# A cap of two on the indirect DMAs under way, and sums in PSUM and sweeps on ScalarE in the last layers of a macaron MoE kernel

## The chip, the cores and the metric

The kernel runs on one core of a Trainium2 chip. The metric is the device time of one execution in microseconds. Twelve runs of the kernel before have a median of 1014.88 us (1011.14 to 1021.59). One further execution was profiled; its lines are what is read below.

The engines are named as the profile names them: PE is TensorE (matmul), PEld its weight load, DVE is VectorE, ACT is ScalarE, POOL is GpSimd, SP is SyncE, which here only issues transfers. An indirect DMA is a transfer whose row numbers are read from a tile; POOL issues it and moves on, and the DMA engines carry it out.

## The reference

The input is 8 batches of 512 tokens with 128 features, all float32. Each token row goes through six residual layers:

```python
x = x + 0.5 * moe(layernorm(x))      # 8 experts, top 2, d_ff 512, relu
x = x + attention(layernorm(x))      # 16 heads of 8, rope, causal, 512 tokens
x = x + 0.5 * moe(layernorm(x))
x = x + 0.5 * fp6_linear(layernorm(x))          # the first fp6 layer
x = x + gated_scan_and_silu_ffn(layernorm(x))   # "mix" below
x = x + 0.5 * fp6_linear(layernorm(x))          # the second fp6 layer
```

`fp6_linear` rounds each block of 32 features to an FP6 grid with one scale per block, multiplies by a quantized 128x128 weight and adds a bias `bq`. `gated_scan_and_silu_ffn` takes u = layernorm(x), normalises it by its root mean square, forms three gates, runs the scan h = a*h + s along the tokens, sets u = u + h, normalises again, and adds a SiLU feed-forward of width 384; the layer's output u + ffn(u) is added to x.

## The kernel before

**Tiles.** A batch is one tile of 128 partitions x 512: four blocks t of 128 tokens, tokens on the partitions and the 128 features along the row. `X[b]` holds the residual of batch b in SBUF from start to end. Eight PSUM banks of 128x512 are shared by everything.

**Mixture of experts.** Stage 0 (before the attention) runs in the groups [0,1], [2,3,4], [5,6,7] of batches, stage 2 (after it) in [0,1], [2,3], [4,5], [6,7]. A group is normalised and routed; POOL then scatters its rows to DRAM, sorted by expert, one indirect DMA per 128 rows and choice (L790, 64 KB each). Expert tiles of 128 rows come back (`xs`), are transposed on PE (L842, `xp`), multiplied by W1 (L853, `hp`), passed through relu (L865, `hs`) and multiplied by W2 (L874, `yp`); DVE adds the bias (L883, `yo`) and SP stores the tile. Each of the 177 tiles loads its expert's weights, 578 KB (L821, `wx`). POOL gathers the results with one indirect DMA per 128 rows and choice (L905, `y`), and DVE adds them to `X[b]` with the gate as weight (L918). There are 128 scatters and 128 gathers.

**Attention.** Scores are formed twice on PE (L1025: `sa` for a maximum that DVE takes at L1077, `sb` for the exponential on ACT at L1088). POOL clears the masked corner (affine select, L1096, `pm`), and PE multiplies by the values (L1132, `av`).

**The tail of a batch** is first fp6 layer, mix, second fp6 layer, and the store of `X[b]` (L1363).

- `normed` (four statistics per tile on DVE at L570, four aggregations at L576, eps added at L577) is followed by a power of -1/2 on POOL (`power`, L588). `scaled_rows` applies it, either on ACT (one DVE product of mean and factor at L599, then four ACT passes of 128x128 at L605) or on DVE (four passes at L609, L611 for the form without a mean).
- `fp6` adds half the bias to `X[b]` (L1267, POOL or DVE), quantizes (`quantized`, L1209 to L1243: twelve DVE or POOL steps, of which L1217, L1233 and L1239 may run on POOL), transposes on PE (L544, `tpq`), copies to SBUF (L531 on ACT, L535 on DVE), multiplies by the weight (L1277, four products into `ypq`) and adds half the product to `X[b]` (L1280, DVE).
- `mix` forms the gates (L1310 on PE, L1312 on ACT), prepares and runs the scan on DVE (L1318, L1320, L1322), transposes h back (four PE transposes at L544 into the bank `ht`), sets u = u + 0.5 h (L1326, DVE), adds u to `X[b]` (L1328, POOL or DVE), normalises u (`root_mean`: four squares on ACT at L556, one DVE step at L559, a power on POOL), and runs the feed-forward (L1337 and L1341 on PE, L1339 on ACT, L1343 on DVE, L1350 on PE into `yom`), whose result DVE adds to `X[b]` (L1356).

**Who sets the order.** Every step is an `Op` with one or more engines that may run it, its estimated costs, the buffers it takes and the steps it needs. `Graph.search` runs a list scheduler 12 times with changing priorities and keeps the best plan; the instructions are then emitted in that order, engine by engine, and each engine's queue runs in the order written. Engines are chosen in the plan, so that a step that may run on POOL or DVE can change sides when anything in the plan changes. `Graph.run` lets at most 8 bulk transfers of a queue be under way; the program itself makes an indirect DMA wait for the one eight before it.

Of the kernel before, what the change touches and what calls it, by code (L numbers as in the profile page):

```python
# [15 lines left out]
P = 128  # L16
# [40 lines left out]
STEP = 4.0  # L57
TURNED = (0,)


# [42 lines left out]
class Op:  # L103

    __slots__ = "alts fn acq bufs deps succ left prio start end eng ready bulk order skew idx pace occ".split()

# [25 lines left out]
class Graph:  # L132
# [4 lines left out]
    def add(self, alts, fn, r=(), w=(), acq=(), deps=(), order=(), bulk=0, skew=0.0, pace=0.0):  # L137
        o = Op()
        o.alts = alts if isinstance(alts, list) else [alts]
        o.fn, o.acq, o.bulk, o.skew, o.pace = fn, list(acq), bulk, skew, pace  # L140
        o.succ, o.start, o.end, o.eng, o.idx = [], None, None, None, len(self.ops)
        needs = {id(d): d for d in deps}
        bufs = {id(b): b for b in acq}
# [25 lines left out]
    def levels(self):  # L169
        for o in reversed(self.ops):  # L170
            e, t, lat, _ = o.alts[0]
            if e == "PE":
                lat = t + 0.3
            if o.bulk:
                lat = 2.2 + o.bulk / 330e3
            o.prio = max(
                [s.prio + (lat if o in s.deps else 0.0) for s in o.succ], default=lat
            ) + o.skew

    def search(self, attending, slots):  # L180
# [18 lines left out]
    def refine(self, order, span, first):  # L199
# [13 lines left out]
        for o, f in zip(self.ops, first):  # L213
            o.prio = MIX * (span - late[id(o)]) + (1 - MIX) * o.prio

    def run(self, attending, slots):
# [46 lines left out]
        while ready:  # L263
            best = []
            low = 1e18
            for o in ready:
# [4 lines left out]
                for alt in o.alts:  # L271
                    e, occ, lat, m = alt
                    st = max(free[e], o.ready, slot_t)
                    if o.bulk and e == "POOL":
                        st = max(st, free[e] + (0.28 if scattering else 0.0))
                    if o.bulk and len(flight[e]) >= 8:
                        st = max(st, flight[e][-8])
                    raw = st
# [68 lines left out]
def kernel(  # L347
# [9 lines left out]
    vecs: bass.AP,  # L357
    bq: bass.AP,
    wq8: bass.AP,
    consts: bass.AP,  # L360
# [125 lines left out]
    half_bq = fixed("half_bq", [P, P])  # L486
    load_late(half_bq, bq.partition_broadcast(P), P * P * 4)
    half_vec = fixed("half_vec", [P, 2])
    wd_t = fixed("wd_t", [P, P])

# [3 lines left out]
    def clear_for_attention(after):  # L494
# [16 lines left out]
        def halves(e):  # L511
            nc.gpsimd.tensor_scalar_mul(half_bq.t, half_bq.t, 0.5)
            nc.gpsimd.tensor_scalar_mul(half_vec.t[:, 0:1], vec_s.t[:, V_BG : V_BG + 1], 0.5)
            nc.gpsimd.tensor_scalar_mul(half_vec.t[:, 1:2], vec_s.t[:, V_BD : V_BD + 1], 0.5)

        add(pool(P, k=2, each=1.3e-3), halves, r=[vec_s], w=[half_bq, half_vec], order=[after])

# [45 lines left out]

    def normed(src, view, name, eps, skew=0.0):

        sm = small(f"sm_{name}")

        def stat(t):
            st = sm.t[:, 0:24].rearrange("p (t k) -> p t k", t=NT)
            nc.vector.bn_stats(out=st[:, t, :], in_=view()[:, t, :])  # L570

        def go(e):
            st = sm.t[:, 0:24].rearrange("p (t k) -> p t k", t=NT)
            mv = sm.t[:, 24:32].rearrange("p (t k) -> p t k", t=NT)
            for t in range(NT):
                nc.vector.bn_aggr(out=mv[:, t, :], in_=st[:, t, :])  # L576
            nc.vector.tensor_scalar_add(sm.t[:, 32:36], mv[:, :, 1], eps)  # L577

        for t in range(NT):
            add(("DVE", 0.2, 0.28, None), lambda e, t=t: stat(t), r=[(src, t)], w=[(sm, t)],  # L580
                acq=[sm] if t == 0 else [], skew=skew)
        add(("DVE", 0.4, 0.5, None), go, w=[sm], skew=skew)
        power(sm, 32, 36, skew)
        return sm
# [51 lines left out]
    def moe_front(s, g):  # L636
# [147 lines left out]
        for n in range(n_b):  # L784
            for k in range(2):
                for t in range(NT):
                    i = n * NT + t

                    def scatter(e, n=n, k=k, t=t, i=i):
# [5 lines left out]
                        )  # L795
                        state["scattered"].append(unordered(ins, f"out{name}"))

                    state["sent"].append(add(
                        ("POOL", 1.02, 2.2, None), scatter, r=[us[n], (keep, f"at{k}"), (rows_in[g], ("s", name, i, k))],
                        bulk=P * P * 4,  # L800
                    ))

    def moe_tiles(s, g):
# [90 lines left out]
    def moe_combine(s, g):  # L894
# [3 lines left out]
        for n, b in enumerate(GROUPS[s][g]):  # L898
            for k in range(2):
                y = buf("g", "y", f"y{k}_{s}_{b}")  # L900
                for t in range(NT):
                    i = n * NT + t

                    def gather(e, y=y, k=k, t=t, i=i):
# [5 lines left out]
                        )  # L910
                        data_from(ins, state["stored"])

                    add(("POOL", 1.02, 2.2, None), gather, r=[(state["keep"], f"at{k}")], w=[(y, t)],
                        acq=[y] if t == 0 else [], deps=state["done"], bulk=P * P * 4)

                def weighed(e, y=y, k=k, n=n, b=b, t=0):
# [343 lines left out]
    def fp6(b, s, sk):  # L1260

        name = f"{s}_{b}"
        y, iz, iv, r = (buf("g", "tail", f"q{k}_{name}") for k in range(4))
        m = normed(X[b], lambda: X[b].t, f"t{name}", 1e-5, skew=sk)
        scaled_rows(y, X[b], lambda: X[b].t, m, acq=[y, iz, iv, r], skew=sk)
        add([pool(S, each=1.7e-3), dve(S, own=True)],
            lambda e: engines[e].tensor_tensor(  # L1267
                X[b].t, X[b].t, half_bq.t.unsqueeze(1).to_broadcast([P, NT, P]), ALU.add),
            r=[half_bq], w=[X[b]], skew=sk)
        quantized(y, iz, iv, r, S // FB, name, small(f"qs_{name}"), skew=sk)  # L1270
# [3 lines left out]

        def go(e):
            for t in range(NT):
                nc.tensor.matmul(yp.t[:, ts(t, P)], iz.t[:, ts(t, P)], wd_t.t, start=True, stop=True)  # L1277

        add(pe(P, NT), go, r=[iz, wd_t], w=[yp], acq=[yp], skew=sk)
        add(dve(S), lambda e: nc.vector.scalar_tensor_tensor(flat(X[b]), yp.t, 0.5, flat(X[b]), ALU.mult, ALU.add),  # L1280
# [5 lines left out]
    def mix(b, sk):  # L1286
        nm = f"{b}"
        u, xn, xnt, s0, s1, s2, h = (buf("g", "tail", f"mix{k}_{nm}") for k in range(7))
        sgs = [s0, s1, s2]
        m = normed(X[b], lambda: X[b].t, f"m{nm}", 1e-5, skew=sk)  # L1290
        scaled_rows(u, X[b], lambda: X[b].t, m, acq=[u, xn, xnt, s0, s1, s2, h], skew=sk)
# [16 lines left out]
        def gate(i, bias, half, n, dst):  # L1308
# [13 lines left out]
        add(dve(2 * S), lambda e: nc.vector.tensor_tensor_scan(h.t, s0.t, s1.t, 0.0, ALU.mult, ALU.add),  # L1322
            r=[s0, s1], w=[h], skew=sk)
        ht = bank(f"ht_{nm}")
        turned(h, lambda: tokens(h), ht, skew=sk)
        add(dve(S), lambda e: nc.vector.scalar_tensor_tensor(u.t, ht.t, 0.5, u.t, ALU.mult, ALU.add),  # L1326
            r=[ht], w=[u], skew=sk)
        add([pool(S), dve(S, own=True)], lambda e: engines[e].tensor_tensor(flat(X[b]), flat(X[b]), u.t, ALU.add),  # L1328
            r=[u], w=[X[b]], skew=sk)
        m2 = root_mean(u, xn, f"n{nm}", 1e-6, skew=sk)  # L1330
# [4 lines left out]
        for f in range(NGF):  # L1335
# [8 lines left out]
                r=[pu], w=[sgs[f]], skew=sk)  # L1344
        yo = bank(f"yom_{nm}")

        def go(e):
            for t in range(NT):
                for f in range(NGF):
                    nc.tensor.matmul(  # L1350
                        yo.t[:, ts(t, P)], sgs[f].t[:, ts(t, P)], wout_s.t[:, f, :],
                        start=(f == 0), stop=(f == NGF - 1),
                    )

        add(pe(P, NT * NGF), go, r=[*sgs, wout_s], w=[yo], acq=[yo], skew=sk)
        add(dve(S), lambda e: nc.vector.tensor_tensor(flat(X[b]), flat(X[b]), yo.t, ALU.add),  # L1356
# [26 lines left out]
    for g in GROUPS[2]:  # L1383
        for b in g:
            tail(b, -STEP * k)
            k += 1

    order = G.search(bursts, SLOTS)
    for o in order:
        for b in o.acq:  # L1390
            where = p_ps if b.kind == "ps" else wk
            b.t = where.tile([P, WIDTH[b.kind]], F32, tag=f"{b.kind}{b.slot}", name=b.name)
        o.fn(o.eng)

# [75 lines left out]
```

## Time and profile before

| | |
|---|---|
| median of 12 runs | 1014.88 us (1011.14 to 1021.59) |
| the profiled execution | 1014.2 us, with a span of 1012.5 us in the trace |
| mean granted clock of TensorE | 0.964 of full speed |
| moved by DMA | 163.61 MB, 162 GB/s mean |
| L905, gathers: one DMA_INDIRECT on POOL | 128 of them, 137.9 us busy |
| L790, scatters: one DMA_INDIRECT on POOL | 128 of them, 131.4 us busy |

The profile's page has the busy time of each engine, the span in 40 slices of 25.3 us with the busy share in tenths, and the chain of work that ended last. Besides the page, four views of the trace are used: the busy time of each engine in chosen stretches of the span; the groups of instructions by line within one stretch; the timeline, instruction by instruction; and the chain in order of time. A group's line gives its count, its busy time in us and the mean ns of one, then the idle time of its engine ahead of it and what ended that.

### The profile page before, as it was taken

How to read it: one execution, taken by the hardware profiler on the slowest of the kernel's cores; microseconds unless marked ns; L12 is line 12 of the kernel's file. 1: busy time of each engine (PE TensorE's matmuls, PEld its weight loads, DVE VectorE, ACT ScalarE, POOL GpSimd, SP SyncE). 2: the span in 40 equal slices, each digit the busy share in tenths (PEclk: the TensorE clock that was granted, in tenths of full speed). 3: DMA queues.
4: the chain of work that ended last, by engine and by line, in shares of the span. 5: the costliest groups of instructions: out<-in, count | busy, mean ns of one | idle time of the engine just before them, and what ended most of it. 6: DMA issues, size and time to landing. Idle time of an engine off the chain costs nothing.

```text
span 1012.5 us, 22544 instructions
## 1 busy us (share of the span) xinstructions
PE 904.5 (89%) x7282; PEld 673.6 (67%) x7282; DVE 739.0 (73%) x2706; ACT 524.6 (52%) x1396; POOL 543.1 (54%) x679
## 2 busy tenths in 40 slices
PE   5488979999999899999999999999998898957973
PEld 5378968776777654656667775665997787534552
DVE  7612364888665699987878668990458869899997
ACT  2144534365666545456656555556555664544641
POOL 3783347267221585475264227783078475775562
PEclk9999998999999979989999999999999999987995
DMA  5779997875554210042343561450899894100001
GB/s 159 263 231 388 361 363 266 285 219 162 181 159 150 70 54 14 22 169 77 117 138 118 151 187 50 147 150 10 278 363 290 266 331 138 34 16 1 22 21 43
DMA packets 102071, 163.61 MB, mean 162 GB/s; under 512 B 11200, under 2 KB 70720, under 8 KB 101952
## 3 DMA queue, kind: packets, MB, share of 16 engines
q1 hardware_dynamic: 93760, 145.37, 43.9%
q0 software_dynamic: 8192, 16.79, 5.0%
q8 instruction: 58, 0.95, 0.4%
q14 instruction: 61, 0.50, 0.1%
HBM read 129.28 MB, written 29.16 MB: 156 GB/s over the span
## 4 chain that ended last, share of the span: by engine, by line
PE 49%; DVE 26%; DMA 8%; POOL 7%; issue 7%; ACT 3%; SPq 1%; POOLq 0%; ACTq 0%; DVEq 0%
PE hp L853 11%; PE yp L874 10%; PE sb L1025 8%; PE sa L1025 7%; PE av L1132 5%; DVE sa L1077 4%; DMA wx<-in_wexp 4%; POOL y L905 3%; DMA y<-rows_out,keep 2%; DVE x L918 2%; POOL rows_in L790 2%; PE lp L670 1%; PE xp L842 1%; DVE q L1241 1%; DVE q L1243 1%
## 5 line engine op out<-in xcount | busy, mean ns | idle before, releaser
L1077 DVE CUSTOM_DVE_ANT_0 sa<-sa,future_s 128x384 f32<-128x384 f32 (+3 forms) x512 | 240.6, 513 | 75.6 <-PE sa L1025 43.8
L865 ACT ACTIVATE hs<-hp,wx 128x128 f32<-128x128 f32 x692 | 196.1, 372 | 141.8 <-PE hp L853 116.2
L1088 ACT ACTIVATE pm<-sb 128x512 f32<-128x512 f32 x320 | 173.2, 598 | 155.5 <-PE sb L1025 79.9
L1096 POOL TENSOR_SCALAR_AFFINE_SELECT pm<-pm 128x256 f32<-128x256 f32 x256 | 107.6, 438 | 190.7 <-ACT pm L1088 189.9
L1025 PE MATMUL sb<-qa,ka 32*128 32x128 f32 (+3 forms) x1024 | 198.8, 467 | 9.0 <-DVE nstat L1077 6.0
L853 PE MATMUL hp<-xt,wx 128*128 128x128 f32 x1416 | 193.7, 283 | 6.4 <-DMA wx<-in_wexp 6.3
L874 PE MATMUL yp<-wx,hs 128*128 128x128 f32 x1416 | 188.2, 278 | 10.4 <-DVE yo L883 8.1
L853 PEld LDWEIGHTS hp<-xt,wx 128*128 128x128 f32 x1416 | 176.4, 196 | 27.5 <-issue 14.5
L1025 PE MATMUL sa<-ka,qm 32*128 32x384 f32 (+3 forms) x1024 | 189.3, 471 | 3.5 <-DVE qm L537 2.3
L874 PEld LDWEIGHTS yp<-wx,hs 128*128 128x128 f32 x1416 | 171.2, 192 | 22.1 <-ACT hs L865 12.3
L905 POOL DMA_INDIRECT y<-rows_out,keep x128 | 137.9, 1078 | 72.3 <-issue 28.8
L790 POOL DMA_INDIRECT rows_in<-um,keep x128 | 131.4, 1027 | 60.3 <-issue 30.6
L1025 PEld LDWEIGHTS sb<-qa,ka 32*128 32x128 f32 x1024 | 100.1, 186 | 46.7 <-DVE nstat L1077 19.0
L1025 PEld LDWEIGHTS sa<-ka,qm 32*128 32x128 f32 x1024 | 87.2, 186 | 28.9 <-issue 3.3
L883 DVE TENSOR_TENSOR yo<-yp,wx 128x128 f32<-128x128 f32 x177 | 49.4, 285 | 65.9 <-PE yp L874 63.7
L1132 PE MATMUL av<-pm,vpad 128*32 128x256 f32 (+3 forms) x1024 | 83.0, 455 | 1.2 <-POOL pm L1096 1.2
L1077 DVE DVE_READ_ACCUMULATOR2_ANT nstat<- 128x1 f32 x512 | 71.5, 140 | 0.0
L1132 PEld LDWEIGHTS av<-pm,vpad 128*32 128x32 f32 x1024 | 29.0, 112 | 60.6 <-issue 38.4
L535 DVE COPY xt<-xp 128x256 f32<-128x256 f32 (+1 forms) x82 | 33.1, 407 | 43.1 <-PE xp L842 43.0
L918 DVE SCALAR_TENSOR_TENSOR x<-y,keep,x 128x128 f32<-128x128 f32 x128 | 49.7, 403 | 14.0 <-DMA y<-rows_out,keep 13.3
L842 PE MATMUL xp<-cst,xs 128*128 128x128 f32 x177 | 35.5, 282 | 13.5 <-DMA xs<-rows_in 12.3
L842 PEld LDWEIGHTS xp<-cst,xs 128*128 128x128 f32 x177 | 22.0, 144 | 18.6 <-issue 14.6
(214 smaller groups left out, 1219.7 us busy)
## 6 DMA issues: line engine op xcount, KB each, us to landing
wx<-in_wexp SPq DMA_DIRECT2D x177, 578.0 KB
xs<-rows_in SPq DMA_DIRECT2D x85, 128.0 KB
rows_out<-yo SPq DMA_DIRECT2D x85, 128.0 KB
rows_in<-zero SPq DMA_DIRECT2D x2, 1984.0 KB
rows_in<-zero SPq DMA_DIRECT2D x2, 1472.0 KB
x<-in_x SPq DMA_DIRECT2D x8, 256.0 KB
rows_in<-um,keep POOLq DMA_INDIRECT x128
y<-rows_out,keep POOLq DMA_INDIRECT x128
```

The costliest lines, as they stand in the source:

```text
L790: ins = nc.gpsimd.indirect_dma_start(out=rows_in[g].t[0 : NTL * TW, :], out_offset=bass.IndirectOffsetOnAxis(ap=at(k)[:, i : i + 1], axis= ...
L842: nc.tensor.transpose(xp.t[:, ts(h, P)], halves(xs.t)[:, h, :], ident)
L853: nc.tensor.matmul(hp.t[:, ts(fc, P)], wx[i].t[:, E_W1 + fc * P : E_W1 + (fc + 1) * P], xt.t[:, ts(h, P)], start=True, stop=True,)
L865: nc.scalar.activation(o, a, AF.Relu, bias=bias)
L874: nc.tensor.matmul(yp.t[:, ts(h, P)], hs[i].t[:, ts(fc, P)], wx[i].t[:, E_W2 + fc * P : E_W2 + (fc + 1) * P], start=(fc == 0), stop=(fc == ...
L905: ins = nc.gpsimd.indirect_dma_start(out=tokens(y)[:, t, :], out_offset=None, in_=rows_out[g].t[0 : NTL * TW, :], in_offset=bass.IndirectO ...
L918: nc.vector.scalar_tensor_tensor(X[b].t[:, t, :], tokens(y)[:, t, :], state["gates"](k)[:, i : i + 1], X[b].t[:, t, :], ALU.mult, ALU.add,)
L1025: nc.tensor.matmul(sc.t[:, at : at + hi - lo], stat.t[rows, ts(m, P)], mov.t[rows, lo:hi], start=True, stop=True,)
L1077: nc.vector.tensor_tensor_reduce(out=sc.t[:, at : at + wd], in0=sc.t[:, at : at + wd], in1=future_s.t[:, S - wd : S], scale=-1.0, scalar=3 ...
L1088: nc.scalar.activation(pm.t[:, (h % 2) * S : (h % 2 + 1) * S], sc.t, AF.Exp, scale=scale)
L1096: nc.gpsimd.affine_select(out=diag, in_=diag, pattern=[[0, 2], [1, P]], compare_op=ALU.is_ge, fill=0.0, base=0, channel_multiplier=-1,)
L1132: nc.tensor.matmul(av.t[32 * j : 32 * j + 32, m * P :], v.t[:, row, :], pm.t[:, at : at + S - m * P], start=first, stop=last,)
```

## The change

**Indirect DMAs.** Every gather, and every scatter but those of the first group of stage 0, is planned with at most two under way (`FLIGHT = 2`), and really waits in POOL's queue for the indirect DMA two before it to have landed.

**Late tails** (batches 4 to 7). In both fp6 layers the bias no longer goes onto `X[b]`: a product of a row of ones with `bq4` (the bias four times, 1x512) opens the bank `ypq`, and the four products accumulate onto it. In the mix, u is put into the bank `ht` by a product of the identity with u (128x512), and four products of h with half the identity accumulate 0.5 h onto it in place of the four transposes; L1326 and L1328 are gone, the second normalisation reads `ht`, the output products (L1350) accumulate onto the same bank, and `X[b]` takes the sum once (L1356). In the first fp6 layer and the mix of these batches ACT, not DVE, adds eps.

**Second fp6 layer** (all eight batches). Mean and variance come from four Copy and four Square passes of ACT with accumulators (`normed_on_act`), one small DVE step before the power and one after it, and four ACT passes apply them (`rows_on_act`). L570, L576, L577 and L599 are gone there.

**The plan** is searched again. `G_BOOST` and `BOOST` hold only zeros. By instructions, from before to after: PE 3940 to 3952, DVE 2708 to 2639, ACT 1366 to 1440, POOL 684 to 668.

```diff
+FLIGHT = 2
+ON_ACT = (5,)
+LATE = (4, 5, 6, 7)
+EPS_ACT = LATE
...
-                    if o.bulk and len(flight[e]) >= 8:
-                        st = max(st, flight[e][-8])
+                    if o.bulk and len(flight[e]) >= o.limit:
+                        st = max(st, flight[e][-o.limit])
...
+bq4 = fixed("bq4", [1, S])
+load_late(bq4, bq4_in, S * 4)
+half_ident = fixed("half_ident", [P, P])
...
+def normed_on_act(src, view, spare, name, eps, acq=(), skew=0.0):
+    sm = small(f"sm_{name}")
+    mean = lambda: mv_of(sm)[:, :, 0]
+    for t in range(NT):
+        add(("ACT", 0.42, 0.55, None), lambda e, t=t: nc.scalar.activation(
+            tokens(spare)[:, t, :], view()[:, t, :], AF.Copy, scale=-1.0 / P, accum_out=sm.t[:, 24 + 2 * t : 25 + 2 * t]),
+            r=[(src, t)], w=[(sm, t), (spare, t)], acq=[sm, *acq] if t == 0 else [], skew=skew)
+    for t in range(NT):
+        add(("ACT", 0.42, 0.55, None), lambda e, t=t: nc.scalar.activation(
+            tokens(spare)[:, t, :], view()[:, t, :], AF.Square, bias=sm.t[:, 24 + 2 * t : 25 + 2 * t],
+            accum_out=sm.t[:, 32 + t : 33 + t]),
+            r=[(src, t)], w=[(sm, t), (spare, t)], skew=skew)
+    add(dve(NT), lambda e: nc.vector.tensor_scalar(
+        sm.t[:, 32:36], sm.t[:, 32:36], 1.0 / P, eps, ALU.mult, ALU.add), w=[sm], skew=skew)
+    power(sm, 32, 36, skew)
+    add(dve(NT), lambda e: nc.vector.tensor_tensor(
+        sm.t[:, 60:64], mean(), sm.t[:, 32:36], ALU.mult), w=[sm], skew=skew)
+    return sm
+
+def rows_on_act(dst, view, sm, skew=0.0, src=None):
+    for t in range(NT):
+        add([("ACT", 0.43, 0.55, None)], lambda e, t=t: nc.scalar.activation(
+            tokens(dst)[:, t, :], view()[:, t, :], AF.Identity, scale=sm.t[:, 32 + t : 33 + t], bias=sm.t[:, 60 + t : 61 + t]),
+            r=[(src, t), sm], w=[(dst, t)], skew=skew)
...
# normed
-            nc.vector.tensor_scalar_add(sm.t[:, 32:36], mv[:, :, 1], eps)
+            if not eps_act:
+                nc.vector.tensor_scalar_add(sm.t[:, 32:36], mv[:, :, 1], eps)
...
+            add(act(NT), lambda e: nc.scalar.activation(sm.t[:, 32:36], mv_of(sm)[:, :, 1], AF.Copy, bias=eps),
+                w=[sm], skew=skew)
...
# scatters, and the same without the condition for gathers
+                    if (s, g) != (0, 0):
+                        state["sent"][-1].limit = FLIGHT
...
# fp6
+            if late:
+                nc.tensor.matmul(yp.t, ones.t[0:1, :], bq4.t, start=True, stop=False, skip_group_check=True)
             for t in range(NT):
-                nc.tensor.matmul(yp.t[:, ts(t, P)], iz.t[:, ts(t, P)], wd_t.t, start=True, stop=True)
+                nc.tensor.matmul(
+                    yp.t[:, ts(t, P)], iz.t[:, ts(t, P)], wd_t.t, start=not late, stop=True, skip_group_check=late)
...
# mix
+            def mixed(e, u=u):
+                nc.tensor.matmul(ht.t, ident, u.t, start=True, stop=False, skip_group_check=True)
+                for t in range(NT):
+                    nc.tensor.matmul(ht.t[:, ts(t, P)], h.t[:, ts(t, P)], half_ident.t,
+                                     start=False, stop=True, skip_group_check=True)
+            u = ht
...
-        yo = bank(f"yom_{nm}")
+        yo = u if late else bank(f"yom_{nm}")
...
# emission
-        o.fn(o.eng)
+        ins = o.fn(o.eng)
+        if o.bulk and o.eng == "POOL":
+            if o.limit < 8:
+                data_from(ins, indirect[-o.limit :][:1])
+            indirect.append(ins)
```

## The prediction

> **What bounds the kernel now.** I read the page's slices first, then the busy times by stretch, then the groups and the timeline of the last stretch.
>
> ```profile
> PE 904.5 (89%) x7282; PEld 673.6 (67%) x7282; DVE 739.0 (73%) x2706; ACT 524.6 (52%) x1396; POOL 543.1 (54%) x679
> ...
> PE   5488979999999899999999999999998898957973
> ...
> DVE  7612364888665699987878668990458869899997
> ```
>
> The mean says PE. The slices say two stages: PE has 9 in nearly all slices from the seventh to the thirtieth, DVE in the last five or six. The table by stretch puts numbers on it (columns: length, then busy PE, PEld, DVE, ACT, POOL; clock, DMA share, GB/s):
>
> ```profile
> 54.00:150.00 96.00, 85.63 (x689) 80.11 (x689) 33.22 (x104) 46.88 (x162) 46.20 (x50) 1.00 0.96 342
> 150.00:420.00 270.00, 261.75 (x2247) 183.78 (x2247) 203.62 (x790) 143.72 (x360) 138.65 (x196) 0.96 0.47 151
> 720.00:860.00 140.00, 129.22 (x1029) 117.73 (x1028) 102.40 (x351) 81.68 (x267) 84.98 (x76) 1.00 0.86 282
> 860.00:1012.50 152.50, 109.48 (x495) 70.68 (x493) 139.54 (x365) 65.99 (x167) 90.84 (x77) 0.86 0.07 23
> ```
>
> Until 860 PE is at 89 to 97% from 54 us on; its idle time there is some 58 us in all, 27 of it in the first 54 us. From 860, when the last expert tile is through, DVE holds the end: 139.5 of 152.5 us. So an edit pays after 860 if it takes DVE time, and costs before 860 if it adds PE time or makes PE wait.
>
> Part of DVE's end stage is not work but stalls beside POOL:
>
> ```profile
> 963.26 1.71 POOL L1328 TENSOR_TENSOR x<-x,mix 128x512 f32<-128x512 f32 x1
> ...
> 963.98 1.28 DVE L1236 TENSOR_SCALAR q<-q 128x512 f32<-128x512 f32 x1
> ...
> 968.21 1.05 POOL L1217 TENSOR_TENSOR q<-q,qs 128x512 f32<-128x512 f32 x1 [0.53 <-DVE qs L1210]
> 968.34 0.95 DVE L577 TENSOR_SCALAR sm_t<-sm_t 128x4 f32<-128x4 f32 x1
> ```
>
> L1236 takes 0.35 us when POOL is quiet and 1.28 beside POOL's addition; the eps step, 0.08 to 0.11 alone, takes 0.95. At each shape's unloaded duration DVE's instructions after the last expert sum come to 115.4 us, against 139.5 busy: 24 us are stalls, over about 35 two-input POOL operations, 0.69 us each. The groups of that stretch show where they land:
>
> ```profile
> L1241 DVE SCALAR_TENSOR_TENSOR q<-q,q 128x512 f32<-128x512 f32 x11 | 9.7, 881 | 1.2 <-POOL q L1239 1.2
> L570 DVE BATCH_NORM_STATS2 sm_t<-x 128x6 f32<-128x128 f32 x36 | 8.9, 276 | 0.0
> L577 DVE TENSOR_SCALAR sm_t<-sm_t 128x4 f32<-128x4 f32 x9 | 6.1, 681 | 0.3
> L1239 DVE TENSOR_TENSOR q<-q,q 128x512 f32<-128x512 f32 x3 | 3.7, 1222 | 0.1
> L1326 DVE SCALAR_TENSOR_TENSOR mix<-ht,mix 128x512 f32<-128x512 f32 x5 | 3.4, 679 | 0.0
> ...
> L1267 POOL TENSOR_TENSOR x<-x,half_bq 128x512 f32<-128x512 f32 x10 | 12.9, 1290 | 10.4 <-ACT q L605 9.4 <-DVE sm_n L559 0.9
> L1239 POOL TENSOR_TENSOR q<-q,q 128x512 f32<-128x512 f32 x8 | 10.5, 1320 | 2.9 <-DVE q L1236 2.8
> ```
>
> **The change part by part.**
>
> *DVE after the last expert sum.* I count instructions in DVE's order behind the last `yo`, before and after the change, at the durations of these groups. Statistics 36 to 11 at 0.25 us (8.9/36): -6.2. Aggregations 36 to 12 at 0.08: -2.0. Eps 13 to 0: -6.8 (6.1 for the fp6 layers, 0.7 for the mix). L599 8 to 2 at 0.245 for the fp6 layers, 5 to 6 for the mix: -1.4. L1326 5 to 0: -3.4. L1328 2 to 0: -1.4. One quantization less behind that point (10 to 9): -5.3. Three L1343, one L1356, one L1280 less: -3.3. Against it: L1239 goes from POOL to DVE, 3 to 9 there, 0.68 us unloaded and 1.22 loaded, +4.1 to +7.3, taken as 5.7; copies L535 0 to 3, +1.8; twelve small steps of the new norm at 0.15, +1.8; L609, L611, L918, L1217, L1233 and L1320 together +1.6. The sum is -18.9. The other way: by unloaded durations the list is 103.5 us instead of 115.4, -11.9, and POOL's two-input operations behind the first gather of that group fall from 36 to 19 (L1267 9 to 2, L1239 7 to 0, L1328 3 to 1, L1233 10 to 8, L1217 7 to 8), 17 x 0.69 = -11.7, together -23.6. If all stalls merely moved to other instructions, only -11.9 would stay. I take -18, with -12 to -24 for the range: when DVE gets thinner its idle time, 9 us of the 149 to its last instruction, grows.
>
> The Trainium skill, "SBUF — State Buffer", section "Who interferes with whom", says that a DVE instruction with two SBUF inputs, or in a two-port mode, contends for a pair of ports with GpSimd, each blocking the other for a whole instruction, and that one with a single SBUF input outside those modes does not. By that rule alone the eps steps, with one SBUF input, would not be held, and taking 13 of them away would be worth 13 x 0.09 = 1.2 us and not 6.8; the row with 681 ns speaks against that, unless such a step runs in one of the two-port modes, which the section does allow it.
>
> *ACT.* For each second fp6 norm ACT gets eight sweeps; L556's, alike, follow each other by 0.29 us: 8 x 0.29 = 2.3 us, where DVE had 4 x 0.20 + 4 x 0.07. In the last stretch six such norms add 14 us and eps some 2 to the 66 of 152: ACT stays at 60%. It lies beside another batch's DVE work, except in the very last tail, where it is in the chain: +1 us (0, or +4 if another tail's eight sweeps and four L605 passes, 2.3 + 1.5, stand ahead of it).
>
> The Trainium skill, "ScalarE: Activation LUTs", gives an ACTIVATE 0.093 us more for each pointer operand. This speaks against the Square and the Identity sweeps; eight such operands more per norm would make 0.7 us more latency each, 0.7 us on the end by its figure.
>
> *PE.* Eight bias products and four identity products of 128x512, 0.95 to 1.02 us each (L1337: 42 records, two a product, in 21.4 us), and sixteen products for sixteen transposes, 0.375 against 0.175 us: +15 us in all. After 860 PE has 43 us idle and this hides there. What counts is the order: at the groups' prices 801.5 us of PE work stood ahead of the last expert product and now 812.1 do, since one batch's feed-forward and products are put ahead. PE's idle time ahead of it can take some; I take +6 (0 to +10.6). DVE work ahead of it is the same, 776.6 and 779.3 us.
>
> *Two indirect DMAs under way.* POOL issues one per 1.30 us and the trace shows how long each flies:
>
> ```profile
> 119.43 1.00 POOL L905 DMA_INDIRECT y<-rows_out,keep  x1 [0.30 <-ACT hs L865]
> ```
> ```profile
> 119.43 6.35 DMA y<-rows_out,keep
> ```
>
> From issue to last packet it is 4.5 to 5.9 us while weights stream (DMA share 0.86 to 1.04) and 1.9 to 2.3 us where DMA is light. With two under way the period is half of that: 2.3 to 3 us loaded instead of 1.3, and still 1.3 when light. Before, four or five flew at once. Queued behind a waiting POOL instruction are the affine selects (L1096, which `av` on PE waits for), powers (L588) and products of the tails. Loaded places: the 16 gathers of stage 0's first group, 114 to 135, which become about 16 x 2.4 = 38 us, so +17 at their end; the 24 scatters at 149 to 184; the scatters and gathers at 736 to 788 and 810 to 834. The last 16 gathers, 866 to 897, run at DMA share 0.07 and are not delayed. PE hides most of it: its order now starts the attention at 127 instead of 107 us of PE work, so the first gathers have 20 us more expert work to hide behind, and the scatters of group 2 are read at 173 instead of 151. The selects have no such cover; I give them 3 us of PE time. Both ends: -2 (the streams of weights get a little more of the wire, 5% of 16 engines' span being indirect) to +16 (nothing hidden at one of the places). I choose near the low end since each place is followed by expert or attention work that PE may take in the written order.
>
> The Trainium skill, "DMA: Bandwidth & Descriptors", section "Anatomy of one DMA", gives 2.0 us plus bytes/436e3 for such a DMA: 2.15 us for 64 KB, so two under way would cost nothing, and this term would be 0. The light rows agree with it; the loaded ones, 6.35 in the chain, do not.
>
> *Fixed costs:* one load of 2 KB and one POOL step more early on, beside streams of 578 KB loads: nothing.
>
> **Sum:** against the profiled execution, 1014.2 - 18 + 1 + 6 + 3 = 1006.2. The median lies 0.7 above that execution; I forecast 1006, with 1000 to 1011 as this case's own range.
>
> **Rivals.**
>
> *The cap starves PE.* At 114 to 150 PE already idles 16% and the whole gain rests on POOL running ahead. If the first gathers' +17 us or the selects behind waiting scatters reach PE, the price is 16 in place of 3 or more, and the end is at 1019; with ACT or the last scatters too, 1023. It decides from the point where POOL's lag passes about 10 us. For it: POOL's waits are real and the planned cost of an indirect DMA is 2.2 us, not 5; PE's order is fixed. Against: the order holds more work ahead of each reader.
>
> *PE becomes the bound and the tail keeps its stalls.* PE gives +10.6, the tail only -12: 1014.2 - 12 + 10.6 + 1 = 1013.8, no difference. For it: L1239 on DVE has two SBUF inputs and meets POOL's L1233.
>
> *The whole tail gain comes, the work ahead is absorbed:* 1014.2 - 24 + 1 + 1 = 992. For it: 17 POOL operations less; PE's 58 us idle.
>
> **How the numbers follow.** My case 0.47; the whole gain 0.15; no difference 0.13; the starved PE 0.25. A measurement tells 0.3% (3 us) from no change. Faster 0.63, same 0.12, slower 0.25. The range leaves out the far parts of both outer cases: 991 to 1021.
>
> **What would show it.** Busy DVE after the last expert sum near 117 to 121 us; L577 gone from the late groups and L1236, L1241 nearer 0.4 and 0.65 us; the last `yp` near 865 (868 or more if the cap costs, 859 if all is absorbed). If indirect DMAs wait long, POOL rows of L790 and L905 show idle time ended by DMA, and PE idle time before `av` ended by POOL's `pm`. I am wrong if PE's idle time ahead of 860 grows by more than 10 us, or if DVE is idle for more than 20 us after it.

## The result

The changed kernel takes 1047.83 us (median of 11 runs, 1040.42 to 1050.43) against 1014.89 us (46 runs): 1.0312 times the time before, 95% interval 1.0293 to 1.0331. I had forecast 1006 us, with a range up to 1021. The profiled execution has a span of 1041.5 us, at a mean granted clock of 0.945 instead of 0.964.

### The profile page after: what moved, and what is told of

The parts are those of the page before. It is cut to its first block, busy times and chain, and to the rows that moved or that the text cites. A ratio compares the mean times of both kernels' runs of the same rounds, so it can differ in the third digit from the quotient of the medians.

```text
span 1041.5 us, 22686 instructions
## 1 busy us (share of the span) xinstructions
PE 920.4 (88%) x7322; PEld 684.2 (66%) x7322; DVE 721.1 (69%) x2637; ACT 548.6 (53%) x1534; POOL 518.9 (50%) x663
## 4 chain that ended last, share of the span: by engine, by line
PE 47%; DVE 17%; DMA 8%; issue 7%; POOL 6%; ACT 3%; SPq 0%; POOLq 0%; DVEq 0%; ACTq 0%
PE yp L925 9%; PE hp L904 9%; PE sb L1078 7%; PE sa L1078 6%; PE av L1185 5%; DVE sa L1130 4%; DMA y<-rows_out,keep 4%; DMA wx<-in_wexp 3%; POOL y L956 3%; ACT pm L1141 1%; DVE x L971 1%; PE xp L893 1%; DVE nstat L1130 1%; DVE q L1287 1%; POOL pm L1149 1%
## 5 line engine op out<-in xcount | busy, mean ns | idle before, releaser
L1078 PE MATMUL sb<-qa,ka 32*128 32x256 f32 (+3 forms) x1024 | 203.1, 479 | 8.5 <-DVE nstat L1130 5.1
L1149 POOL TENSOR_SCALAR_AFFINE_SELECT pm<-pm 128x256 f32<-128x256 f32 x256 | 105.1, 429 | 203.6 <-ACT pm L1141 202.5
L1078 PE MATMUL sa<-ka,qm 32*128 32x384 f32 (+3 forms) x1024 | 192.8, 488 | 2.8 <-DVE nstat L1130 2.5
L925 PE MATMUL yp<-wx,hs 128*128 128x128 f32 x1416 | 186.5, 277 | 5.1 <-DVE yo L934 4.9
L956 POOL DMA_INDIRECT y<-rows_out,keep x128 | 137.0, 1070 | 99.7 <-DMA wx<-in_wexp 34.2
L1078 PEld LDWEIGHTS sb<-qa,ka 32*128 32x128 f32 x1024 | 102.5, 191 | 47.4 <-DVE nstat L1130 15.6
L1078 PEld LDWEIGHTS sa<-ka,qm 32*128 32x128 f32 x1024 | 90.5, 195 | 29.0 <-DVE nstat L1130 6.6
L971 DVE SCALAR_TENSOR_TENSOR x<-y,keep,x 128x128 f32<-128x128 f32 x128 | 49.3, 389 | 63.3 <-DMA y<-rows_out,keep 63.1
L1185 PE MATMUL av<-pm,vpad 128*32 128x256 f32 (+3 forms) x1024 | 85.5, 465 | 4.3 <-DVE nstat L1130 2.6
L550 DVE COPY xt<-xp 128x256 f32<-128x256 f32 (+1 forms) x87 | 35.5, 408 | 37.7 <-PE xp L893 37.0
```

Of the source, the lines that this page charges most:

```text
L925: nc.tensor.matmul(yp.t[:, ts(h, P)], hs[i].t[:, ts(fc, P)], wx[i].t[:, E_W2 + fc * P : E_W2 + (fc + 1) * P], start=(fc == 0), stop=(fc == ...
L956: ins = nc.gpsimd.indirect_dma_start(out=tokens(y)[:, t, :], out_offset=None, in_=rows_out[g].t[0 : NTL * TW, :], in_offset=bass.IndirectO ...
L971: nc.vector.scalar_tensor_tensor(X[b].t[:, t, :], tokens(y)[:, t, :], state["gates"](k)[:, i : i + 1], X[b].t[:, t, :], ALU.mult, ALU.add,)
L1078: nc.tensor.matmul(sc.t[:, at : at + hi - lo], stat.t[rows, ts(m, P)], mov.t[rows, lo:hi], start=True, stop=True,)
L1149: nc.gpsimd.affine_select(out=diag, in_=diag, pattern=[[0, 2], [1, P]], compare_op=ALU.is_ge, fill=0.0, base=0, channel_multiplier=-1,)
L1185: nc.tensor.matmul(av.t[32 * j : 32 * j + 32, m * P :], v.t[:, row, :], pm.t[:, at : at + S - m * P], start=first, stop=last,)
```

## The profile after

The page's engine line and two rows of its 40 slices:

```profile
PE 920.4 (88%) x7322; PEld 684.2 (66%) x7322; DVE 721.1 (69%) x2637; ACT 548.6 (53%) x1534; POOL 518.9 (50%) x663
...
PE   6389289987999989999999999999999888958995
...
PEclk9999699968999999889999999999999999979995
```

PE's fifth slice, 104 to 130 us, stands at 2; the fifth slice of before had 9, and the granted clock drops in the same slice and again in the ninth. The table by stretch (columns as before; the last row begins where the last expert product ends), and the row of the kernel before from its last expert product on:

```profile
54.00:150.00 96.00, 69.92 (x554) 65.61 (x553) 24.34 (x81) 38.89 (x135) 43.93 (x50) 0.89 0.85 285
...
902.00:1041.50 139.50, 108.41 (x469) 68.41 (x467) 113.03 (x296) 74.47 (x253) 67.89 (x59) 0.86 0.07 24
```
```profile
862.60:1012.50 149.90, 106.88 (x477) 68.70 (x476) 137.09 (x358) 64.14 (x163) 90.02 (x76) 0.86 0.07 23
```

The last expert product ends at 902.0 us, before at 862.6: 39.4 us later. From there to the end it takes 139.5 us, before 149.9: 10.4 us less. So the tail is faster, and all of the loss and more lies ahead of it. In the 39 us PE idles 25 us more (90.0 against 65.0 us up to that product) and is busy 14 us longer (812.0 against 797.6). Of the idle time 16 us come before the attention's first score, which starts at 185.4 instead of 149.9 us; the rest of that delay is the 20 us of expert work that the new order puts ahead of the attention.

The 16 us come with one gap of 20.65 us; before, no gap of PE between 104 and 150 us is longer than 2.3 us. PE's timeline, then SP's in the changed kernel, SP's first load of the same rows in the kernel before, and POOL's in the changed kernel:

```profile
101.42 1.95 PE L925 MATMUL yp<-wx,hs 128*128 128x128 f32 x16
124.02 1.11 PE L893 MATMUL xp<-cst,xs 128*128 128x128 f32 x4 [20.65 <-DMA xs<-rows_in]
```
```profile
106.07 0.43 SPq L427 DMA_DIRECT2D wattn_s<-in_wattn  x1
...
107.69 0.55 SPq L478 DMA_DIRECT2D rows_in<-zero  x1
108.28 9.57 SPq L427 DMA_DIRECT2D half_bq<-in_bq  x1
...
119.50 1.93 SPq L882 DMA_DIRECT2D xs<-rows_in  x4
...
134.93 2.23 SPq L872 DMA_DIRECT2D wx<-in_wexp  x2
```
```profile
94.14 0.38 SPq L831 DMA_DIRECT2D xs<-rows_in  x1
```
```profile
82.10 0.98 POOL L838 DMA_INDIRECT rows_in<-um,keep  x1 [0.30 <-issue]
83.39 0.98 POOL L838 DMA_INDIRECT rows_in<-um,keep  x1 [0.30 <-issue]
```

PE waits for the rows of the second group (`xs`). SP loads them only at 119.5 us, behind a block of constants and the clear of the third group's rows, during which one issue holds the queue for 9.57 us. No weights are issued from 106 to 135 us either. The rows had been there long before: POOL still issued that group's scatters every 1.29 us, as before, with packets ending about 5 us after each issue, and the last ended at 89.8 us. So the scatters of a group do not wait for the one two before: the program declares them independent of each other, and the instructions of one group carry no such wait. The plan counts them as capped, so it must place their landing later, and SP's order is filled with other loads ahead of them; that this is what moves SP's order is tried below (e6, e11).

The gathers do wait. What ended POOL's idle time ahead of L956 (the gathers; us, times), who waited for them, and DVE's wait for gathers in the kernel before (L918):

```profile
  DMA y<-rows_out,keep: 26.5, 27
...
  DVE x L971: 63.1, 47
```
```profile
  DMA y<-rows_out,keep: 13.3, 15
```

Ahead of its weighted sums DVE waits 63.1 us for gathers; before it was 13.3 us.

## The experiments

Ratios are to the kernel before, run beside each kernel on the same chip; two kernels are compared on one chip where that is possible. The chips are not alike: e1 to e12 ran on chips where the kernel before takes 1015 to 1018 us (e1 to e4 on one, e5 to e8 on a second, e9 to e12 on a third), e13 to e16 and e17 to e18 on two where it takes 1091 and 1103 us (see the last section).

### The cap: its plan and its waits apart

`e1_nocap` takes the cap out of both, `e2_plan2_nowait` leaves the plan and drops the waits, `e3_plan8_wait2` plans without it and keeps the waits, `e4_before_cap` puts the cap into the kernel before.

```diff
# e1 (and e12, e17)
-FLIGHT = 2
+FLIGHT = 8
# e2
-            if o.limit < 8:
-                data_from(ins, indirect[-o.limit :][:1])
# e3
-                    if o.bulk and len(flight[e]) >= o.limit:
-                        st = max(st, flight[e][-o.limit])
+                    if o.bulk and len(flight[e]) >= 8:
+                        st = max(st, flight[e][-8])
# e4: the diff's lines on FLIGHT and limit, on the kernel before
```

> The changed kernel with FLIGHT = 8: no cap in the plan and no added wait; the late tails and the ACT norms stay. Theory P (the cap as the plan sees it moves the order, above all constants and a clear ahead of the rows of the second group on SP): PE's idle gap near 104 to 124 us goes and the time is 1000 to 1012 us. Theory W (the real waits of the gathers): also 1000 to 1012 us. Theory T (the new tails' products and sweeps cost the time): 1035 us or more still.

> The changed kernel with its plan as it is, order unchanged, but without the added waits on the indirect DMA two before. P: 1035 to 1048 us, since the order is the same; the gap near 104 us stays at 15 to 21 us. W: 1005 to 1020 us. T: 1035 to 1048 us.

> The changed kernel planned without the cap, but with the added waits. P: within 5 us of the kernel with neither (1000 to 1015 us). W: 1030 to 1045 us. T: 1035 us or more.

> The kernel before with the cap alone, in plan and waits; its tails are as before. P and W: 1035 to 1060 us, since the tail's gain of some 10 us is missing too. T: 1015 us or within 5 us of it.

| | median us | ratio (95%) |
|---|---|---|
| e1, neither | 1007.63 | 0.9901 (0.9864 to 0.9939) |
| e2, plan only | 1038.45 | 1.0211 (1.0170 to 1.0252) |
| the changed kernel, both | 1047.83 (not beside these) | 1.0312 (1.0293 to 1.0331) |
| e3, waits only | 1057.90 | 1.0369 (1.0316 to 1.0423) |
| e4, both, tails as before | 1050.23 | 1.0320 (1.0254 to 1.0385) |

T falls: without the cap the new tails are faster than the kernel before. P and W each had half: the plan alone costs 31 us, the waits alone 50 us, and together they cost 4.1% of 1015, or 42 us. In the order of the capped plan the waits add only 10 us, not 50, and that order loses 31 us by itself. On the tails as before the cap costs 32 us (e4).

Both halves can be followed in the traces up to the last expert product. The capped order of e2 has PE's gap too (20.86 us), and PE idles 86.9 us up to that product, against 66.6 in e1. In e3 PE idles 106.7 us, 40 more than in e1; 20 of these come before the attention's first score and 20 behind it.

What the waits do is seen in e3, whose order on DVE, ACT and POOL is that of e1, instruction by instruction. Its sixteen first gathers are issued from 112.9 to 153.6 us, 2.7 us each, where e1 has 112.1 to 132.0, 1.3 each. DVE's and PE's waits there (the waits of DVE in 110 to 160 us, then PE's timeline):

```profile
DVE x L971 <- DMA y<-rows_out,keep: 15.2, 6, 3.9
DVE u L657 <- POOL sm_a L636: 10.4, 1, 10.4
```
```profile
142.65 2.05 PE L925 MATMUL yp<-wx,hs 128*128 128x128 f32 x8 [11.79 <-DVE yo L934]
...
156.08 1.24 PE L559 MATMUL tpa<-cst,u 128*128 128x128 f32 x4 [8.46 <-DVE u L657]
```

Two roads lead from a waiting gather to PE. DVE's weighted sums stand in its queue ahead of `yo`, and PE's next `yp` needs the bank that `yo` frees: 11.8 us. And a power on POOL, queued behind the waiting gathers, holds a normalisation (L657): 8.5 us. Over the whole run PE waits 31.3 us for `yo`, in e1 8.1.

### How many under way

`e7_plan8_wait4` waits for the gather four before, in e1's order.

```diff
# on e3
-                data_from(ins, indirect[-o.limit :][:1])
+                data_from(ins, indirect[-4:][:1])
```

> The plan without the cap, with a real wait on the indirect DMA four before instead of two before. Theory L (what costs is the flight time of 4.5 to 5.9 us over the number under way, against 1.3 us of issue): the period is 1.2 to 1.5 us and the time 1005 to 1015 us. Theory S (each added wait costs by itself): 1035 us or more, as with two.

1014.74 us, 1.0000 (0.9974 to 1.0026). The sixteen gathers take 24.0 us from the first issue to the last, 1.6 each, and still fly 4.7 to 6.2 us. So the order is eight, four, two: 1.3, 1.6, 2.7 us a gather and 0.990, 1.000, 1.037 in time. That is about L, the flight time over the number under way, though 1.6 us lies above the 1.2 to 1.5 that I expected. The time of e7 is scattered (1007 to 1019, and the profile is of the fastest run), and the part between e1 and e7 is the less certain one.

### Which transfers' cap

```diff
# e6: scatters planned with eight
-                        state["sent"][-1].limit = FLIGHT
+                        state["sent"][-1].limit = 8
# e11: gathers planned with eight, and without the wait
-                    o.limit = FLIGHT
+                    o.limit = 8
```

> The changed kernel with the cap on the gathers alone, in plan and waits; the scatters are planned with eight. Theory A (a plan that knows of the waits of the gathers hides them): 1005 to 1020 us, with SP's early order as without a cap. Theory B (real waits cost about 50 us in any order that puts DVE's weighted adds ahead of other work): 1035 to 1060 us.

> The changed kernel with the cap on the scatters alone. In the program a scatter waits for the one two before only where another group's transfer stands there, since scatters of one group are declared independent; so this is nearly the plan's side alone. Theory Q (the plan's cost comes from scatters that the plan believes slow): 1025 to 1040 us. Theory R (it comes from the gathers' side, or from both together): 1003 to 1015 us, with SP's early order as without a cap.

e6: 1056.37 us, 1.0414 (1.0334 to 1.0493). A falls. The time lies in B's range, but B's road is not what the trace shows: PE waits 4.8 us for `yo`, against 31.3 in e3. Beside e1 the last expert product ends 35 us later (894.3 us), with 13 us more idle time of PE and 22 us more busy time at a lower clock (0.929 on the mean, 0.83 from 150 to 300 us), and the stretch behind it takes 164.6 us instead of 145.3. No run has e6's plan without its waits, so how much of the 5% is the order and how much the waits stays open.

e11: 1030.41 us, 1.0142 (1.0103 to 1.0181), 2.2% over the uncapped kernel on the same chip (0.9923). Q holds: PE's gap is there again, from 103.1 to 125.7 us behind `xs`, with a cap that the scatters hardly feel, and SP has the same block of constants and the clear ahead of the rows. In e6, where the plan sees the scatters free, SP loads that group's rows from 91.8 us on between the weights, and the gap is gone. So it is what the plan believes of the scatters that moves SP's order, and most of the plan's cost (22 of 31 us, across two chips) comes with it.

### The front of SP's order

`e5_late_consts` and `e9_late_halves` edit the finished order of e2.

```diff
# e5
+    at = order.index(rows_1[3])
+    order = [o for o in order[: at + 1] if o not in back] + back + order[at + 1 :]
# back: loads of constants and the clear that stood ahead of the fourth row load of group 1
# e9: behind the eighth row load, and the halving of the constants (POOL) behind the 16 first gathers
```

> The plan of the changed kernel without the added waits, with one edit of the order: the constants' loads and the clear of the third group's rows stand behind the first four loads of the second group's rows in SP's queue, not ahead of them. Theory P1 (that place of SP's order makes the PE gap of 21 us at 104 and most of the plan's cost): the gap shrinks below 5 us and the time is 1015 to 1025 us, 15 to 21 less than the 1038 of the same plan. Theory P2 (the plan is late in many places, and the gap only takes up what would be lost later): 1030 to 1040 us although the gap is gone.

> The plan of the changed kernel without the added waits, with two edits of the order: the constants' loads and the clear stand behind the first eight row loads of the second group on SP, and the halving of the constants stands behind the sixteen gathers of the first group on POOL. In the run with the first edit alone the gap of 21 us became three of 8, 5 and 8, the second and third of which stood behind DVE copies queued behind weighted sums that waited for gathers behind the halving. Theory P1 (this chain SP, POOL, DVE, PE makes the gap): the idle time of PE in 54 to 150 us falls from 23 to 5 to 12 us and the time to 1018 to 1030 us. Theory P2 (PE's order after it makes up the loss anyway): still 1034 to 1042 us.

e5: 1042.13 us, 1.0283 (1.0228 to 1.0338). The gap is split, not gone: 8.4 us behind `xs`, then 5.1 and 7.9 behind `xt` copies on DVE. These stand behind weighted sums that wait for gathers: the first two gathers of the group in one case, in the other gathers queued behind the halving on POOL, which waits for `half_bq` behind the clear on SP. e9: 1045.07 us, 1.0275 (1.0231 to 1.0320): 8.5 us behind `xs`, 2.7 behind `xt`, and 9.2 behind weights, since SP reaches the next weights only at 138.1 us. P1 as I stated it falls; the idle time is the same 21 us in all three. SP has one long stretch without weights, and moving pieces within it changes only what PE waits for.

The other way of taking it away is to plan the front as without a cap: `e13_front_free`, and `e18_front_free` beside a base, `e17_nocap_base`.

```diff
# on e2
-                    if (s, g) != (0, 0):
+                    if (s, g) not in ((0, 0), (0, 1)):
```

> The changed kernel without the added waits, planned with the cap everywhere but on the scatters of the second group of stage 0. Theory F (the front of SP's order carries the plan's cost): the attention starts before 155 us as without a cap, and the time is 1005 to 1020 us, against 1038 with the cap there. Theory G (the capped plan is late all along): the attention starts early and the time is still 1028 to 1040 us.

> The changed kernel without the cap as a base: 0.988 to 0.994 of the kernel before where that takes some 1017 us; where it takes 1091 us, 0.995 to 1.003, as with the waits on the last gathers alone, if those cost nothing.

> The changed kernel without the added waits, planned with the cap everywhere but on the scatters of the second group of stage 0, once more. Theory F (the front of SP's order carries the plan's cost): within 1% of the base, and where the kernel before takes some 1017 us, 1005 to 1018 us and no gap of PE over 5 us between 90 and 150 us. Theory G (the capped plan is late all along): 1028 us or more there.

e13: 1085.53 us, 0.9935 (0.9912 to 0.9958). e18: 1094.58 us, 0.9958 (0.9917 to 0.9999), beside e17 with 1097.06 us, 0.9957 (0.9913 to 1.0001). With the cap in the whole plan but for the scatters of one group, the kernel is as fast as without any cap, and SP loads that group's rows between the weights again (in e18 from 114.7 us on). This speaks for F, against the 3.1% between e1 and e2, but does not show it: the kernel with the cap on that group was not run on these chips, where PE idles for weights in that stretch anyway (e17 in the last section), so the capped order may cost less there too. The attention started at 203 to 205 us, not before 155 as I had expected, and the first sixteen gathers are spread from 134 to 208 or 210 us: the searched order differs from e17's in more than SP's front.

### Where the waits cost

`e14_wait_first` and `e15_wait_last` put the waits on sixteen gathers only, in e1's order.

```diff
# on e3, scatters at eight
-                    o.limit = FLIGHT
+                    o.limit = FLIGHT if (s, g) == (0, 0) else 8   # e15: (2, 3)
```

> The uncapped plan, order unchanged, with the real waits on the sixteen gathers of the first group of stage 0 alone, while weights stream. Theory L (flight time over the number under way, passed on by DVE's weighted sums to PE): the sixteenth gather is issued some 20 us later, the attention starts at 165 to 175 instead of 150 us, and the time is 1020 to 1032 us. If the waits cost mostly elsewhere: 1006 to 1015 us.

> The same with the waits on the sixteen gathers of the last group of stage 2 alone, where the DMA engines are light and a gather flies 1.9 to 2.3 us. Theory L: nothing, 1003 to 1012 us. Theory S (a wait costs by itself): 1013 us or more.

e14: 1098.93 us, 1.0069 (1.0042 to 1.0096); e15: 1095.45 us, 1.0004 (0.9970 to 1.0038), on one chip. The first gathers run from 134.8 to 175.0 us in e14 and from 134.2 to 153.8 in e15, 20 us longer as L said, and the attention starts at 192.9 and 183.9 us. At the end it is 3 us by the medians and 0.65%, 7 us, by the ratios: less than expected, on a chip where PE idles for weights in that stretch anyway. e15 cannot be told from the base (0.9957, on another chip), so whether the last waits cost nothing or a few us stays open.

### The parts of the tail

```diff
# e8: late sums alone        # e10: second norms on ACT alone
-FLIGHT = 2                  -FLIGHT = 2
+FLIGHT = 8                  +FLIGHT = 8
-ON_ACT = (5,)               -LATE = (4, 5, 6, 7)
+ON_ACT = ()                 +LATE = ()
-EPS_ACT = LATE              -EPS_ACT = LATE
+EPS_ACT = ()                +EPS_ACT = ()
# e16: FLIGHT = 8 and EPS_ACT = () alone
```

> The kernel before with the late tails' sums in PSUM alone: no cap, no norms or eps on ACT. If the gain of the tail (10 us without the cap) comes from the bias and the additions taken off POOL and DVE: 1006 to 1010 us. If it comes from the norms on ACT: 1013 to 1017 us.

> The kernel before with the second fp6 norms on ACT alone: no cap, no late sums, eps on DVE. If the norms carry the tail's gain: 1003 to 1010 us. If gains need both, so that neither alone moves the time: 1012 to 1018 us.

> The changed kernel without the cap once more, for a narrower interval, beside the parts: 1003 to 1010 us, 0.987 to 0.994 of before.

> The changed kernel without the cap, with eps on DVE again; late sums and second norms on ACT stay. By the eps steps' own row (13 late ones, 6.8 us with their stalls) it is 5 to 7 us slower than with eps on ACT: 1012 to 1016 us. If the stalls moved on to the next instruction: 1007 to 1010 us.

e8: 1017.66 us, 1.0021 (0.9996 to 1.0046). e10: 1014.31 us, 0.9979 (0.9952 to 1.0006). e12, all three parts, beside e10: 1007.64 us, 0.9923 (0.9893 to 0.9953). e16: 1096.89 us, 1.0030 (1.0001 to 1.0058), where all parts have 1.0004 (e15, on the same chip, the order of e1 with the waits on the last sixteen gathers) and 0.9957 (e17, on another). Neither of the two parts alone can be told from no change, and together with eps they give 0.8 to 1.0% on the faster chips. The last expert product ends at 871 us in e8, at 863 in e10, and at 859 and 866 in e1 and e12, which are one program in one order: executions differ by 7 us, each set of parts has an order of its own, and both move the time by as much as the parts do. How the gain divides stays open. e1, at 1007.6 us, is the version that beats both kernels.

## Why the prediction was wrong, step by step

**What bounds the kernel** was right: PE until the last expert product, DVE after it. PE's idle time before 860, which I put at some 58 us, is 65 by the rows that I used. Both signs of being wrong that I had named came: PE's idle time ahead of the last product grew by 25 us, and DVE is idle for 26.5 us after it.

The profiled execution is 29.0 us longer than the one before. Up to the last product PE idles 25.0 us more and is busy 14.4 us longer; the stretch behind it is 10.4 us shorter. My sum had +3 and +6 in place of the first two, and -18 + 1 in place of the third.

**DVE after the last expert sum: -18 (-12 to -24).** This term was too large. In the changed kernel the work went as counted. From the last product to the end DVE is busy 113.0 us instead of 137.1, 24 less; the eps step of L577 is gone from the late batches, and the groups of DVE in the last stretch of the changed kernel (902 us on) show it:

```profile
L1342 DVE SCALAR_TENSOR_TENSOR x<-ypq,x 128x512 f32<-128x512 f32 x11 | 7.5, 681 | 6.6 <-PE ypq L1338 6.6
...
L1294 DVE SCALAR_TENSOR_TENSOR q<-q,q 128x512 f32<-128x512 f32 x9 | 6.1, 683 | 0.0
...
L1289 DVE TENSOR_SCALAR q<-q 128x512 f32<-128x512 f32 x9 | 4.5, 501 | 0.1
...
L1277 DVE TENSOR_SCALAR q<-q 128x512 int32<-128x512 int32 x9 | 4.0, 443 | 3.6 <-POOL q L1270 3.6
```

L1294 (before L1241) takes 683 ns instead of 881, L1289 (L1236) 501 instead of 600. But the stretch is only 10.4 us shorter, outside my range, since DVE's idle time in it, 12.8 us before, is now 26.5: for `ypq` 6.6 instead of 3.7, for POOL's L1270 3.6, for gathers 4.4. In e1, without the cap, the stretch is 145.3 us against 149.9, and DVE's busy time in it (124.7 us from 860 on) only 12 less than before: in that order one quantization more stands behind the last product, and small steps are long (L647 642 ns, L574 442, where L599 and L559 before took 148 and 155). Between my two sums and the value I took lay 1 to 6 us for such idle time, and it grew by 14.

**ACT +1, PE +6.** ACT is busy 53% of the last stretch; I said 60%. The eight sweeps of one norm take 2.8 us in the last tail (1014.7 to 1017.5 us), half a us more than I counted. PE's 14.4 us more of busy time go with a lower clock: the granted clock is 0.80 from 114 to 150 us and 0.80 from 200 to 250, where it was 1.00 before. Weighted at each moment with the granted clock, PE's busy time up to the last product is 782 us before and 783 now, an estimate from the clock records of the two traces; two kernels with one order, e1 and e3, give 771 us both, at 792.8 and 806.3 us busy. So the work that I priced at +6 does not show there, and the lower clock, some 14 us, had no term in my sum. Without the cap's term my sum is 1014.2 - 18 + 1 + 6 = 1003.2, a gain of 11 us; e1 and e12 gained 0.99% and 0.77%, 8 to 10 us. That this comes close owes something to luck: the tail of e1 gave 4.5 us, not 18, and its last product did not end 6 us later but 3 us earlier (4 later in e12).

**Two indirect DMAs under way: +3 (-2 to +16).** This is the step that failed. The cap costs 42 us, the lower clock and the changed tail included, and my bounds did not hold it. Three things in it were wrong.

- I took the plan's answer to the cap as cover ("its order now starts the attention at 127 instead of 107 us of PE work, so the first gathers have 20 us more expert work to hide behind"). I read that from PE's order alone. SP's order had the rows of the second group behind a block of constants and a clear, which takes the rows from under that very work: PE idled 20.65 us, and the plan alone costs 31 us (e2). It comes with the plan's cap on the scatters (e11 against e6); that SP's front alone carries it is likely from e13 and e18, which ran on other chips, and not shown.
- I gave the scatters a real wait. Those of one group have none; they run every 1.29 us as before. The plan's belief in it, not the wait, was the cost.
- For the gathers the period under load was right (2.7 us in e3 against my 2.3 to 3). The powers queued behind them on POOL I named and did not price (8.5 us of PE in e3). I left out who waits for the gathers: DVE's weighted sums, and behind them in DVE's queue `yo` and `xt`, so PE. In an order that does not know of the waits they cost 50 us (e3).

The rival "the cap starves PE" had half of the mechanism, the waits, and not the order of SP's queue. I priced it at 16 us because I let one stage pay for it; in e3 half of PE's added idle time lies behind the first stage, and it is paid in two queues, POOL's and DVE's.

## What to carry to other kernels

A limit given to a planner changes what it believes about landings, and with that the order of the queues. Read the new order of the queue that loads things (here SP's) next to the bound engine's, and ask of each moved block which rows or weights come after it. In this kernel a real limit on transfers set their period to about the flight time over the number under way (e3, e7), and it was paid by whoever stands in the queue behind the first consumer, here DVE's sums, as well as behind the issuer. A gain at the end of a kernel is worth what the stretch loses in length, not what its engine loses in busy time.

## What the runs showed of the hardware

The issue after a clear of the gathered rows (1984 KB in one transfer) held SP for 7.7 to 9.6 us, with two kinds of load: `half_bq`, 64 KB, 9.57 us in the changed kernel and 7.65 in e5 (0.47 in the kernel before, where it stood elsewhere); the weights behind the same clear 9.47 us for a pair in the kernel before and 9.05 in e1. SP stands still at other places too (a pair of row loads took 10.50 us in e1 at 149 us, eight took 13.50 in e9), and why is not seen.

The same kernel took different times on different chips: e1 and e17 are one program in one order, 1007.6 and 1097.1 us. Three chips gave the shorter time of the kernel before, two the longer one, which were also used later; the chip and the hour are not told apart. They part where the first weights stream (54 to 114 us, e1 and then e17):

```profile
54.00:114.00 60.00, 56.55 (x471) 55.07 (x470) 13.77 (x43) 30.13 (x108) 26.46 (x31) 1.00 0.93 334
```
```profile
54.00:114.00 60.00, 39.35 (x272) 36.40 (x271) 7.97 (x25) 17.94 (x64) 25.05 (x29) 0.80 0.57 190
```

The DMA engines move 334 and 190 GB/s, busy 93% and 57%. PE's work there then comes later, and the attention starts at 186.5 instead of 149.7 us. The ratio of two kernels differs too (0.990 in e1, 0.992 in e12, 0.996 in e17, with intervals that overlap), so a comparison across the two kinds of chip, even by ratios, is no more than a hint.
